# Another share of the work by seven products in the first two blocks of an RWKV layer and its feed-forward layer on Trainium2

## The chip, the cores and the metric

The kernel runs on one core of a Trainium2 chip. The metric is the device time of one execution in microseconds (us). The core's engines appear in the profile as PE (TensorE, matrix products and transposes), PEld (its weight loads), DVE (VectorE), ACT (ScalarE), POOL (GpSimd) and SP (SyncE, which only issues DMAs here). DMAs are also issued on ACT's and POOL's queues.

## The reference

All is fp32, on x with 2048 tokens of 512 numbers. First comes an RWKV layer on the layer norm of x, added to x, then a feed-forward layer on the layer norm of that, added too.

```
z  = layernorm(x)
h  = layernorm(z) * g1 + b1;  hh = h moved by one token
k, v, r = mix_k(h, hh) @ Wk.T, mix_v(h, hh) @ Wv.T, mix_r(h, hh) @ Wr.T
x1 = z + (sigmoid(r) * wkv(k, v)) @ Wo.T           # time mix
h  = layernorm(x1) * g2 + b2; hh = h moved by one token
x2 = x1 + sigmoid(mix_cr(h, hh) @ Wcr.T) * (silu(mix_ck(h, hh) @ Wkey.T) @ Wval.T)   # channel mix
y  = x + x2
out = y + (silu(gate) * up) @ w_down.T,  gate, up = split(layernorm(y) @ w_gate_up.T)
```

Wk, Wv, Wr, Wo and Wcr are 512 x 512, Wkey is 2048 x 512 and Wval 512 x 2048; the feed-forward layer is 2048 wide. mix is `h*m + hh*(1-m)` with one m for each feature.

## The kernel before

The 2048 tokens are four blocks of 512. A block's product with a 512 x 512 piece of weights is a **unit**. There are two kinds. `plain_unit` (L636) makes 32 matmuls of 128 x 128 by 128 x 256, in four quads of eight, from the weights as they lie in memory. `unit` (L541) works by seven products of half size (Winograd's form of Strassen's algorithm), 7 x 4 = 28 matmuls at L560; for this it needs four sums of weight quarters (S1 to S4) and four sums of operand quarters (T1 to T4, `sums_of`, L466, on DVE) and puts the products together with copies on ACT (`accv` L580, `u` L591, `accx` L595) and additions on DVE. An fp32 matmul leaves two records on PE in the trace. The last three products of a unit are `held`: the unit that follows pops them between its own. A plain unit with `hold` leaves its last two quads in the same way.

The weight sums are made once, in the background, by `prepare` (L147): four loads of quarters on POOL's queue (L152), four operations on DVE (L389), and behind each a write of the sum to DRAM on POOL's queue (L163). The quarters lie either in `q` buffers (30 of them, which the units use too) or in six `raw` buffers of their own. `prepare_all(weights, own, depth)` gives the order; with depth 2 the next weight's quarters are loaded while the one before is summed, with depth 1 only behind it. PE's operands come through a ring of twelve buffers that SP's queue fills in the order of use (`ring`, L166, L168), weights and sums alike; a read of a sum that isn't written yet holds up all reads behind it.

The order of PE, DVE and ACT is written out when the kernel is built, by a small planner. After every product `tick` (L297) adds share x 1.72 us to an account (`slack`) and lets background work run until the estimated DVE cost of it (`cost`, L208) has used the account up. Background work is norms, mixes and residuals, pushed as generators, and the steps of `prepare`, which are paced by `credit`: each tick adds `credit[1]`, and each step costs 1. `share` is SHARE0 up to the first up unit and SHARE behind it. So a larger share or credit moves instructions forward on all three engines, whether or not what they wait for comes sooner.

Norm 1, the time-mix norm of the second block, is `time_norm(1)` (L757): moments on DVE (L403, L404), variance and a column `shift` (L393, L397), `pow` on POOL (L413), four h on DVE (L393), then sixteen transposes on PE (L445) and ACT's evacuations to hT. For blocks 2 and 3 the norm is done on transposed input (`turned_norm`, L783): the statistics go to DRAM (L795), come back as rows by two DMAs on ACT's queue (L804), DVE applies them to xT (L389), and ACT writes hT (L816).

The units run in this order: k, r, v, out of block 0; k, r, v of block 1; then for each block b gate, out of block b+1, four up units, one down unit over the four pieces of Wval, and k, r, v of block b+2; then the feed-forward layer (gate, up and down units, L1214 among them). k, r, v and out of block 0 and k of block 1 are plain. `first_block` (L824) starts with norm 0 and its transposes, behind 24 transposes that warm PE up (L345).

Of the kernel before, what the change touches and what calls it, by code (L numbers as in the profile page):

```python
# [22 lines left out]
WAIT = 5  # L23
STEP = 1.72
SHARE = 0.88
SHARE0 = 0.95
WARM = 24
PP0 = -1e38

# [4 lines left out]
WK, WV, WR, WO, WCR = range(5)  # L34

TURNED = 2
PLAIN = {(0, WK), (0, WR), (0, WV), (0, WO), (1, WK)}
WKEY = 5
WVAL = 9
WG = 13  # L40
# [22 lines left out]
def rwkv_ffn_kernel(  # L63
# [32 lines left out]
    def q_tile(name):  # L96
        return pools["q"].tile([P, 2, HB], F32, tag="q", name=name)
# [49 lines left out]
    def prepare(n, own):  # L147

        raw = []
        for k in range(4):  # L150
            t = prep.tile([P, 2, HB], F32, tag="raw", name="raw") if own else q_tile("q")
            paced(nc.gpsimd.dma_start(flat(t), sources[n][k]))  # L152
            raw.append(t)
        yield 1
        a11, a12, a22, a21 = raw
        for k, o, i0, i1, op in (
            (0, a22, a21, a22, ALU.add),
            (2, a21, a11, a21, ALU.subtract),
            (1, a11, a22, a11, ALU.subtract),
            (3, a12, a12, a11, ALU.subtract),  # L160
        ):
            tt(o, i0, i1, op)
            nc.gpsimd.dma_start(sums[n][k], flat(o))  # L163
            yield
# [37 lines left out]
    slack = [0.0]  # L202
    share = [SHARE0]
    put_off = deque()
# [6 lines left out]
    def later(fn, ticks=1):  # L211
        put_off.append([ticks - 1, fn])
# [4 lines left out]
    def flush():  # L217
        while put_off:
            flush_one()
# [31 lines left out]
    credit = [0.0, 0.0]  # L251
# [17 lines left out]
    def begin(item):  # L269
        if not item[4]:  # L270
            item[4] = True
            next(item[2])
            item[1] = WAIT

    def prepare_all(ns, own, depth):
        empty = not preps
        for n in ns:
            preps.append([n, 0, prepare(n, own), depth, False])
        if empty:
            for item in list(preps)[:depth]:  # L280
                begin(item)
# [34 lines left out]
    def push(name, gen, ready=None):  # L316
        background.append([ready, gen, name, False, background])
# [4 lines left out]
    def need(name):  # L322
        while name not in finished:
            run_one(True)
        slack[0] = min(slack[0], 0.0)
        spent[0] = 0.0
# [61 lines left out]
    def tt(out, a, b, op):  # L388
        nc.vector.tensor_tensor(out, a, b, op)  # L389
        cost(size(out))  # L390

    def ts(out, *args):
        nc.vector.tensor_scalar(out, *args)  # L393
        cost(size(out), 0.1, 0.00085)

    def stt(out, *args):
        nc.vector.scalar_tensor_tensor(out, *args)  # L397
        cost(size(out))
# [89 lines left out]
    def mix(key, hT, row, plain=False):  # L488
        m, B = op_tile("mix")
        B["key"] = key  # L490
        ops[key] = B

        def dst(c):
            k = c // 2
            return m[:, 2 * k : 2 * k + 2, c % 2, :]

        def shifted(c):
            nc.scalar.activation(
                dst(c),
                hT[:, c, 0:TB].rearrange("p (j t) -> p j t", j=2),  # L500
                AF.Copy,
                scale=onem[:, row - MK, c : c + 1],
            )

        def mixed(c):
            stt(
                dst(c),
                hT[:, c, 1:].rearrange("p (j t) -> p j t", j=2),
                vcol(row, c),
                dst(c),  # L510
                ALU.mult,
                ALU.add,
            )

        shifted(0)
        shifted(1)
        yield 1
        for c in range(NC):
            mixed(c)
            if c + 2 < NC:  # L520
                shifted(c + 2)
            yield
        finished.add(B["key"])
        if not plain:
            yield from sums_of(B)
# [188 lines left out]
    def product_of(b, n, name, sink, by_token, done=None, free=op_done):  # L714
        if (b, name) not in ops:
            flush()
        plain = (b, n) in PLAIN
        B = Lazy((b, name), plain)
        if name != "g":
            need((b, name))  # L720
        if plain:
            plain_unit(
                n,
                B,
                sink,
                by_token,
                done,
                free,
                second_half if (b, name) == (0, "k") else None,
                (b, n) == (1, WK),  # L730
            )
        else:
            unit([n], [B], sink, by_token, done, free)
# [176 lines left out]
    def time_mix(b, name):  # L910
        row, n = {"k": (MK, WK), "r": (MR, WR), "v": (MV, WV)}[name]
        yield from mix((b, name), hTs[b, "a"], row, (b, n) in PLAIN)

# [8 lines left out]
    def k_unit(b):  # L922
        q = qs[b] = {}

        def sink(i, j, c):
            r = q_tile("r")
            for o in range(2):
                n = 2 * i + o

                ts(r[:, o, :], c[:, o, :], nfirst[:, n : n + 1], 0.0, ALU.subtract, ALU.min)  # L930
            e = q_tile("e")
            q[i, j] = e
            nc.scalar.activation(e, r, AF.Exp)
            nc.scalar.activation(r, r, AF.Exp, scale=-1.0)


            later(lambda: stt(e, e, 0.5, r, ALU.mult, ALU.mult), 2)

        product_of(b, WK, "k", sink, False)
# [20 lines left out]
    def v_unit(b):  # L960
# [5 lines left out]
        def done():  # L966
            hidden_sums((b, "g"), q, (b, WO) in PLAIN)

        product_of(b, WV, "v", sink, False, done)

    def block_view(t, i, j):
        return t[:, 2 * j : 2 * j + 2, i * HB : (i + 1) * HB]

    def out_unit(b):
        need(("x1", b))

        def sink(i, j, c):
            v = block_view(x1s[b], i, j)
            tt(v, c, v, ALU.add)

        product_of(b, WO, "g", sink, True, free=None)
# [5 lines left out]
    def channel_norm(b):  # L987
        x1 = x1s[b]
        mv = small.tile([P, NT, 2], F32, tag="mv", name="mv")
        yield from moments(x1, mv)  # L990
        var = small.tile([P, NT], F32, tag="var", name="var")
        ts(var, mv[:, :, 1], EPS, None, ALU.add)
        rstd = small.tile([P, NT], F32, tag="rstd", name="rstd")
        yield from rsqrt(var, rstd, NT, b == 0)
        h = tok_tile("h")
        yield from scaled(x1, h, mv, rstd)
        hT = htp.tile([P, NC, TB + 1], F32, tag="hT", name="hT_b")
        hTs[b, "b"] = hT
        yield 1
        yield from shifted_norm("b", h, hT, LN2G, LN2B)  # L1000
# [322 lines left out]

    early = [WR, WV, WCR, WO] + [WKEY + g for g in range(4)] + [WVAL, WVAL + 1]
    late = [n + g for g in range(4) for n in (WG, WU)] + [("dd", A11)]
    late += [("d", k) for k in range(4)] + [("dd", q) for q in (S4, S2, A12, S1, S3, A22)]

# [5 lines left out]
    second_half = first_block()  # L1335
    for n in "rv":
        push_mix(0, n, time_mix(0, n))
    credit[1] = 0.65
    k_unit(0)
    prepare_all(early, False, 2)  # L1340
    prepare_all([WVAL + 2, WVAL + 3] + [WK] + late, True, 1)
    xin[1] = load_x(1)
    push("norm1", time_norm(1))
    push_residual(0)
# [3 lines left out]
    r_unit(0)  # L1348
    v_unit(0)
    out_unit(0)  # L1350
    push("normb0", channel_norm(0))
    k_unit(1)
    push_mix(0, "cr", channel_mix(0, "cr"))
    push_mix(0, "ck", channel_mix(0, "ck"))
    r_unit(1)
# [1 line left out]
    for b in range(NB):  # L1357
        nxt = b + 2 < NB
        if nxt:
            xin[b + 2] = load_x(b + 2)  # L1360
        if b == NB - 1:
            load_resid(0)
        gate_unit(b)
        if b + 1 < NB:
            out_unit(b + 1)
        need((b, "ck"))
        if nxt:
            push(f"norm{b + 2}", time_norm(b + 2))
        for g in range(4):
            up_unit(b, g)  # L1370
            if b == 0:
                share[0] = SHARE
            if b == 1 and g == 0:
                credit[1] = 0.55
            if g == 0:
                if nxt:
                    push_mix(b + 2, "k", time_mix(b + 2, "k"))
                    push_residual(b + 2)
                    push_mix(b + 2, "r", time_mix(b + 2, "r"))
                if b + 1 < NB:  # L1380
                    push(f"normb{b + 1}", channel_norm(b + 1))
                if nxt:
                    push_mix(b + 2, "v", time_mix(b + 2, "v"))
                if b + 1 < NB:
                    push_mix(b + 1, "cr", channel_mix(b + 1, "cr"))
                    push_mix(b + 1, "ck", channel_mix(b + 1, "ck"))
        if b == NB - 1:
            push((0, "z", "t"), ffn_in(0), op_free)
        down_unit(b)
        if nxt:  # L1390
            for n, u in (("k", k_unit), ("r", r_unit), ("v", v_unit)):
                u(b + 2)
# [95 lines left out]
```

## Time and profile before

| | |
|---|---|
| three runs | 1239.46, 1239.35, 1240.74 us |
| median of the runs | 1239.46 us |
| profiled execution | 1238.08 us |
| its span in the trace | 1236.0 us |
| mean granted TensorE clock | 0.999 |
| DMA traffic | 294.06 MB, HBM at 237 GB/s |

The profile shows one execution of its own. The span is the time from the first to the last instruction in the trace; 2.08 us lie around it. Line numbers (L560) are those of the kernel below or above in this section; the form `out<-in` names the program's tiles. A row of a timeline has the start in the span, the time of the group, engine, line and operation, and in brackets the idle time of the engine ahead of it with what ended it.

### The profile page before, as it was taken

The numbers are of one execution on the slowest core, as the hardware profiler recorded it, in microseconds if no ns is written. First come the engines' busy times: TensorE is split into PE (matmuls) and PEld (weight loads), VectorE is DVE, ScalarE is ACT, GpSimd is POOL, SyncE is SP. The second block draws the span as 40 slices with busy tenths as digits, with TensorE's granted clock in tenths as the row PEclk, the third lists the DMA queues.
The fourth block names the chain that finished last, engine by engine and source line by source line (L and its number), as shares of the span: only waits on it lengthen the run. The fifth ranks groups of instructions, "written<-read, shape, count | busy, mean of one in ns | idle before, by whom it ended". The sixth has DMA issues, their size and how long they took to land.

```text
span 1236.0 us, 18098 instructions
## 1 busy us (share of the span) xinstructions
PE 1226.3 (99%) x6516; PEld 1099.8 (89%) x6516; DVE 714.4 (58%) x1321; ACT 359.3 (29%) x666; POOL 154.4 (12%) x278
## 2 busy tenths in 40 slices
PE   9999999999999999999999999999999999999998
PEld 8888887888888888888888888998899888998898
DVE  5888587586684757533532365556546365563466
ACT  5534252242522425202211222112221222112211
POOL 2332321222212121222000000000000000000000
PEclk9999999999999999999999999999999999999999
DMA  5779985899877887898556645895459745785576
GB/s 201 253 261 315 340 278 208 307 325 311 274 243 250 293 271 238 262 324 301 176 145 194 213 140 160 269 335 152 142 183 311 269 145 150 239 296 160 153 216 211
DMA packets 140303, 294.06 MB, mean 238 GB/s; under 512 B 17576, under 2 KB 18744, under 8 KB 138936
## 3 DMA queue, kind: packets, MB, share of 16 engines
q1 hardware_dynamic: 117168, 219.99, 56.3%
q0 software_dynamic: 21440, 70.27, 15.6%
q10 hardware_dynamic: 1608, 2.65, 0.6%
q8 instruction: 53, 0.87, 0.3%
q14 instruction: 34, 0.28, 0.1%
HBM read 250.89 MB, written 41.95 MB: 237 GB/s over the span
## 4 chain that ended last, share of the span: by engine, by line
PE 92%; issue 3%; DMA 2%; POOL 2%; DVE 1%; ACT 0%; POOLq 0%; DVEq 0%; ACTq 0%
PE ps L560 52%; PE ps L1214 14%; PE accx L560 10%; PE accv L560 10%; PE ps L662 4%; PE ps L445 1%; POOL q L152 1%; DMA row<-stats 1%; POOL sum L163 1%; DMA w<-sum 0%; DMA sum<-q 0%; DMA x<-in_x 0%; DVE h L393 0%; DVE resid L389 0%; DVE r L389 0%
## 5 line engine op out<-in xcount | busy, mean ns | idle before, releaser
L560 PE MATMUL ps<-zT,w 128*128 128x256 f32 x1280 | 289.5, 379 | 0.0
L560 PEld LDWEIGHTS ps<-zT,w 128*128 128x128 f32 x1280 | 241.9, 190 | 32.2
L560 PE MATMUL ps<-mix,w 128*128 128x256 f32 x960 | 219.7, 379 | 0.5 <-ACT u L591 0.5
L560 PEld LDWEIGHTS ps<-mix,w 128*128 128x128 f32 x960 | 182.1, 190 | 25.5 <-ACT u L591 0.9
L389 DVE TENSOR_TENSOR u<-u,accx 128x512 f32<-128x512 f32 x67 | 46.0, 686 | 120.5 <-ACT accx L595 120.4
L560 PE MATMUL ps<-w,t 128*128 128x256 f32 x456 | 102.5, 379 | 2.2 <-DVE st L403 1.8
L1214 PE MATMUL ps<-w,hid 128*128 128x128 f32 x832 | 104.5, 275 | 0.0
L1214 PEld LDWEIGHTS ps<-w,hid 128*128 128x128 f32 x832 | 99.8, 192 | 0.8
L560 PEld LDWEIGHTS ps<-w,t 128*128 128x128 f32 x456 | 86.2, 190 | 14.5 <-DVE st L403 2.1
L580 ACT COPY accv<-ps 128x512 f32<-128x512 f32 x67 | 38.2, 571 | 177.2 <-PE ps L560 177.2
L1214 PE MATMUL ps<-w,quads 128*128 128x128 f32 x704 | 89.0, 275 | 0.4 <-ACT r L1226 0.4
L1214 PEld LDWEIGHTS ps<-w,quads 128*128 128x128 f32 x704 | 84.2, 192 | 0.9 <-ACT r L1226 0.5
L595 ACT COPY accx<-ps 128x512 f32<-128x512 f32 x67 | 38.2, 571 | 153.6 <-PE ps L560 153.6
L389 DVE TENSOR_TENSOR u<-ps,u 128x512 f32<-128x512 f32 x67 | 46.2, 690 | 61.8 <-PE ps L560 61.5
L591 ACT COPY u<-ps 128x512 f32<-128x512 f32 x67 | 39.2, 585 | 123.4 <-PE ps L560 123.4
L1308 POOL DMA_DIRECT2D out<-resid x12 | 8.6, 716 | 512.1 <-DVE resid L389 512.1
L389 DVE TENSOR_TENSOR raw<-raw 128x512 f32<-128x512 f32 x88 | 60.5, 687 | 20.4 <-DMA raw<-in_wd 10.5
L1226 ACT COPY r<-ps 128x128 f32<-128x128 f32 x112 | 29.8, 266 | 142.1 <-PE ps L1214 142.1
L560 PE MATMUL accv<-zT,w 128*128 128x256 f32 x256 | 60.6, 379 | 0.0
L560 PE MATMUL accx<-zT,w 128*128 128x256 f32 x256 | 60.5, 379 | 0.0
L560 PE MATMUL ps<-w,s 128*128 128x256 f32 x256 | 58.2, 379 | 0.0
L662 PE MATMUL ps<-mix,w 128*128 128x256 f32 x256 | 56.8, 380 | 1.1 <-DVE mix L397 1.1
(168 smaller groups left out, 1658.8 us busy)
## 6 DMA issues: line engine op xcount, KB each, us to landing
w<-sum SPq DMA_DIRECT2D x316, 256.0 KB, 3.5
w<-in_w SPq DMA_DIRECT2D x253, 256.0 KB, 3.7
w<-dd SPq DMA_DIRECT2D x112, 256.0 KB, 3.7
w<-d SPq DMA_DIRECT2D x48, 256.0 KB, 3.7
raw<-in_w POOLq DMA_DIRECT2D x44, 256.0 KB, 5.7
sum<-raw POOLq DMA_DIRECT2D x44, 256.0 KB, 3.9
q<-in_w POOLq DMA_DIRECT2D x40, 256.0 KB, 5.9
sum<-q POOLq DMA_DIRECT2D x40, 256.0 KB, 4.5
```

Source lines behind the costliest of these rows:

```text
L152: paced(nc.gpsimd.dma_start(flat(t), sources[n][k]))
L163: nc.gpsimd.dma_start(sums[n][k], flat(o))
L389: nc.vector.tensor_tensor(out, a, b, op)
L445: nc.tensor.transpose(flat[:, t * P : (t + 1) * P], h[:, t, c * P : (c + 1) * P], ident)
L560: mm = nc.tensor.matmul(pz[:, m, :], lhsT=lhsT, rhs=rhs, start=first and g == 0 and m == 0 and k == 0, stop=g == last and k == 1, skip_gro ...
L580: "z", A11, B11, True, pop_held, read=lambda: nc.scalar.copy(accv, acc["z"])
L591: nc.scalar.copy(tmp["u2"], acc["z"])
L595: nc.scalar.copy(accx, acc["z"])
L662: mm = nc.tensor.matmul(acc[i, j][:, m, :], lhsT=act[:, k, lo] if by_token else wg[:, k, lo], rhs=wg[:, k, :] if by_token else act[:, k, : ...
L1214: mm = nc.tensor.matmul(dst, lhsT=x[k][:, g, :], rhs=wt[:, g, :], start=first and g == 0, stop=g == 3, skip_group_check=True,)
L1226: nc.scalar.copy(st["r"][:, m, n * P : (n + 1) * P], st["z"])
L1308: eng.dma_start(out_t[b][:, tokens, cols], rs[b][:, tokens, cols])
```

## The change

Six places are edited. SHARE0 goes from 0.95 to 1.05. k of block 1 leaves the set of plain units, and out of block 0 now has the hold. WK's sums are made first instead of behind those of Wval, and three pieces of Wval instead of two are summed in q buffers with depth 2; only the fourth goes through the `raw` buffers. The credit of a tick in the first part is 0.75 instead of 0.65, and 0.72 instead of 0.75 from the first up unit of block 0 on, where before it stayed at 0.65; from block 1's first up unit it is 0.55 as before. The channel norm of block 0 is pushed behind k of block 1 instead of ahead of it.

```diff
-SHARE0 = 0.95
+SHARE0 = 1.05
...
-PLAIN = {(0, WK), (0, WR), (0, WV), (0, WO), (1, WK)}
+PLAIN = {(0, WK), (0, WR), (0, WV), (0, WO)}
...
                 second_half if (b, name) == (0, "k") else None,
-                (b, n) == (1, WK),
+                (b, n) == (0, WO),
...
-    early = [WR, WV, WCR, WO] + [WKEY + g for g in range(4)] + [WVAL, WVAL + 1]
+    early = [WK, WR, WV, WCR, WO] + [WKEY + g for g in range(4)] + [WVAL + g for g in range(3)]
...
-    credit[1] = 0.65
+    credit[1] = 0.75
     k_unit(0)
     prepare_all(early, False, 2)
-    prepare_all([WVAL + 2, WVAL + 3] + [WK] + late, True, 1)
+    prepare_all([WVAL + 3] + late, True, 1)
...
     out_unit(0)
+    k_unit(1)
     push("normb0", channel_norm(0))
-    k_unit(1)
...
             if b == 0:
                 share[0] = SHARE
+                if g == 0:
+                    credit[1] = 0.72
```

## Prediction

> **What bounds the kernel now.** I read the page's busy times first, then the waits of PE and of SP's queue, then PE's timeline around each wait, and last the chain of waits.
>
> ```profile
> PE 1226.3 (99%) x6516; PEld 1099.8 (89%) x6516; DVE 714.4 (58%) x1321; ACT 359.3 (29%) x666; POOL 154.4 (12%) x278
> ```
>
> PE is busy 1226.3 of 1236.0 us, so an edit counts only where it changes PE's work or makes PE wait. Adding up the idle time ahead of PE's groups after the start leaves five places: 0.34 us at 28.1 (a mix), 0.46 at 42.85 (norm 1), 0.7 at 161.6 (block 2's k), and 1.93 and 0.65 at 201.6 and 205.7, where the first down unit lacks the sums of its fourth value block. Some 4.2 us is all that better timing can win. In the waits of PE and of SP's queue the largest of these and its cause stand as:
>
> ```profile
> PE ps L560 <- DVE st L403: 1.8, 1, 1.8
> ```
>
> ```profile
> SPq L168 <- DMA sum<-raw: 31.4, 3, 13.7
> ```
>
> The columns are total, count, longest. PE's wait is put down to a DVE operation that was long done; the SP row names the real one. The ring's reads stood up to 13.7 us behind one write of sums.
>
> **The sum goes against the profiled execution**, 1238.08 us (span 1236.0 and 2.08 around it), which lies 1.38 under the median of the runs, 1239.46. I work out a difference and add it to the median.
>
> **A. k of block 1 by seven: −1.73.** A plain unit is 32 matmuls and a unit of seven products 28. Each fp32 matmul has two records on PE.
>
> ```profile
> 46.95 29.36 PE ps L662 x136
> ```
>
> In this piece of the chain PE ran 136 records in 29.36 us without a break, 0.2159 us each. The change replaces 64 such records by 56: 8 × 0.2159 = 1.73 less. The unit's additions (four T, the u copies and additions, all on DVE and ACT) lie beside PE, which is ahead of them by its own units as in every other unit of seven. The hold moves to out of block 0: its last two quads are spread over k's products, the same matmuls in another order, so nothing. WK's sums are made first: four reads and four writes on POOL's queue, written by about 40 us and read by SP from about 66 us on. Three more loads pass SP's ring, 3 × 3.5 us landing, behind twelve buffers: nothing. The sums behind WK (r, v, cr, out, the first keys) come up to 12 us later than before and, in the instruction order, still at least 12 us ahead of their reads: nothing, and a few tenths if that cover fails.
>
> **B. The larger share moves norm 1's transposes: +4.1.** With SHARE0 at 1.05 the planner gives background work more room per product, and time_norm(1) reaches its transposes (L445) two steps of the planner earlier. PE's order is fixed when the kernel is built: the first four transposes now stand directly behind the last matmul of r of block 0, eight matmul pairs (16 records, 3.45 us) earlier than before. What they wait for does not come earlier. PE's timeline, then DVE's, then POOL's:
>
> ```profile
> 42.85 1.50 PE L445 MATMUL ps<-ident,h 128*128 128x128 f32 x8
> 44.19 1.89 PE L662 MATMUL ps<-mix,w 128*128 128x256 f32 x8
> ```
>
> ```profile
> 37.88 0.24 DVE L393 TENSOR_SCALAR var<-mv 128x4 f32<-128x4 f32 x2
> ...
> 40.41 1.00 DVE L393 TENSOR_SCALAR h<-x,mv,two 128x512 f32<-128x512 f32 x2 [0.22 <-POOL two L413]
> ...
> 42.53 1.00 DVE L393 TENSOR_SCALAR h<-x,mv,two 128x512 f32<-128x512 f32 x2
> ```
>
> ```profile
> 38.21 2.17 POOL L413 TENSOR_TENSOR two<-var,mhalf 128x8 f32<-128x8 f32 x1 [7.97 <-DVE shift L397]
> ```
>
> Up to var (37.88) DVE's order is unchanged and DVE is fully busy, so the chain var, pow on POOL (2.17), first h at 40.41 stands. In the new order DVE then does one h (0.46), one e (0.60), two sums of weights (0.60 and 0.72) and three more h (0.46, 0.46, 0.54): 40.41 + 3.84 = 44.25; the last transpose of the first four, which reads the fourth h, starts at about 44.29. PE is there at 39.40 (end of r's last matmul in before). Three transposes are done inside the wait (3 × 0.11): 44.29 − 39.40 − 0.33 = 4.56. Before, the same place cost 0.46, so +4.1. Queued behind the waiting transposes is all of v's first quad, and nothing gives it back: DVE's lead over PE grows by 4 us, but PE is the bound. If the 0.34 at 28.1 goes, PE only comes to this wait earlier. The orders are fixed, so only the durations can vary: bounds 3.5 (DVE 0.6 sooner, one operation) and 4.6 (all of the wait is new).
>
> **C. The clock: +2.0, bounds 0 and 2.8.** A wait of over 4 us on PE is not in the trace after the start; the longest, 1.93 us, left the granted clock at 1.00. Near rows stand at the two ends of the run. From the windows of granted clock (the column after DVE, ACT and POOL), after PE's last matmul, which ends at 1232.03:
>
> ```profile
> 1232.00:1233.00 1.00, 0.03 (x1) 0.00 (x0) 0.84 (x2) 0.00 (x0) 0.00 (x0) 1.00 0.00 0
> ...
> 1234.00:1235.00 1.00, 0.00 (x0) 0.00 (x0) 0.00 (x0) 0.00 (x0) 0.00 (x0) 0.66 0.38 114
> 1235.00:1236.00 1.00, 0.00 (x0) 0.00 (x0) 0.00 (x0) 0.00 (x0) 0.00 (x0) 0.50 0.00 0
> ```
>
> The clock is at a half 2.3 us after PE stopped. So a wait of 4.6 us is long enough, and work behind it would begin at half speed. The price is read at the start:
>
> ```profile
> 1.37 4.84 PE L345 MATMUL warm<-ident 128*128 128x128 f32 x24 [1.37 <-POOL ident masks.py:199]
> 6.04 1.06 PE L351 MATMUL accv<-ident 128*128 128x128 f32 x8
> ```
>
> Eight transposes of one shape later take 1.06 us, so one is (1.06 − 0.275) / 7 = 0.112 behind the other (0.275 is the mean of one). 24 would be 23 × 0.112 + 0.275 = 2.85, and took 4.84: 2.0 us lost until the clock was up. That is the value I take, since it is the only warming in the trace. Zero if the clock holds; half of the 5.5 us from the span's start until full pace, 2.8, if it rises late.
>
> By the Trainium skill ("TensorE: Matmul & The Clock Gate", Why this matters for your kernels) PE should have no idle gap over about 3 us, since one idle window brings the clock to a half; its Part 1 gives a window of some 3.4 us. This rule speaks against the change, and the trace's end agrees with it. One such window at half speed would lose about 1.7 us, an estimate from that page, and the sum below would be 0.3 lower.
>
> **D. Three value blocks in the q buffers: −2.58.**
>
> ```profile
> 194.52 5.34 PE L560 MATMUL ps<-w,t 128*128 128x256 f32 x24
> 201.63 1.97 PE L560 MATMUL ps<-w,t 128*128 128x256 f32 x8 [1.77 <-DVE st L403]
> ...
> 205.74 6.50 PE L560 MATMUL ps<-w,t 128*128 128x256 f32 x29 [0.41 <-DMA w<-sum]
> ```
>
> ```profile
> 196.59 0.54 POOL L163 DMA_DIRECT2D sum<-raw  x1 [4.84 <-DVE raw L389]
> ```
>
> PE is through 24 records at 194.52 + 24 × 0.2159 = 199.70 and goes on at 201.63, 1.93 later; 0.08 and 0.57 follow (205.17 against 205.74). The third sum of the fourth value block is written at 196.59 and reaches its matmul 5.04 later, at 201.63. With the third block in the q buffers the fourth one's quarters are loaded before the third one's sums are written, and in the new order this write is issued 6 planner steps after the down unit starts instead of 11, about 10.4 us instead of 19.0. Its matmul is due 22.4 us after that start; 10.4 + 5.0 = 15.4 leaves 7 us. All 2.58 goes, and nothing else is late there. Bounds −2.58 and 0.
>
> **E. The statistics rows of block 2: +0.8, bounds −0.7 and +2.3.** In before the rows are issued at 147.48 and land 7.3 and 9.2 us later; PE waits 0.7 at 161.61.
>
> ```profile
> 147.48 0.85 ACTq L804 DMA_DIRECT2D row<-stats  x2
> ...
> 308.28 0.84 ACTq L804 DMA_DIRECT2D row<-stats  x2
> ```
>
> The new order puts both of ACT's first hT evacuations (L816) ahead of its accv copy (L580) of the unit that PE is in, so rows, xT on DVE, hT, accv, PE hang in one line. Block 3 has this order already: rows issued 308.28, xT at 313.69 and 314.97 (6.3 us), accv copied by ACT at 317.75, PE at 318.38 where 318.30 was due: no wait. With 9.2 us it would be 2.9 of wait. In the middle (7.75) it is 1.5; less the 0.7 paid now, +0.8.
>
> The first channel norm behind k starts some 4 us later; its transposes stand as many products ahead of the gate as before (DVE has one operation less between), and POOL's pow and DVE are not behind there because PE's wait in B lets them catch up: nothing, bounds 0 and 0.7. DVE is about full from 66 to 92 us (26.3 us of work in 25.9).
>
> **The sum**: −1.73 + 4.1 + 2.0 − 2.58 + 0.8 = +2.6. The profiled execution would be 1240.7, the median 1239.46 + 2.6 = 1242.1. About 0.2%, 2.48 us, is what a measurement can tell from no change, so the bounds are 1236.98 and 1241.94.
>
> **Rivals.** 1. Not slower: the clock holds through B's wait. For it: waits of up to 1.93 us did not lower it. Against it: it was down 2.3 us after PE's end. It decides at a wait somewhere between 1.9 and 4.6 us. C is 0: +0.6, 1240.1, with −0.7 in E 1238.5. Chance 0.28. 2. Faster: B does not happen since the h are ready when the transposes come. All four would have to end by 39.4, 4.8 us earlier than worked out; POOL's spans are rough, but the first h at 40.41 is a DVE record. −1.73 − 0.46 − 2.58 + 0.8 = −4.0, 1235.5. Chance 0.06. 3. The rows land at 9.2 us and more: +1.4 on the forecast, and if the clock is the upper bound 0.8 more: 1243.5 to 1244.4. Chance 0.14. 4. The change does not do what it says: the fourth value block is still late, +2.6: 1244.7. Chance 0.05. The forecast itself, 1241 to 1243, keeps 0.47.
>
> **The numbers.** 1238.5 to 1245 leaves out rival 2 and about 0.08 of the others. Faster is rival 2 alone, 0.06. Rival 1 and a little under half of the forecast lie within 0.2%: 0.46. The rest is slower, 0.48.
>
> **What would show it.** A: L662 has 64 records fewer, L560 56 more. B: PE's first group on L445 behind 39 waits 4 to 5 us for h on L393. C: the granted clock in the windows from 42 to 48 is under 1.00. D: no wait of PE between 190 and 210, and SP's row on sum<-raw far under 13.7. E: PE waits 0 to 3 us for ACT behind the rows at about 160. The prediction is wrong if PE waits anywhere else after 48 us by over 1 us, or if the transposes' wait is under 3 us.

## The result and the profile after

Five runs of the changed kernel gave 1244.30 to 1246.42 us, median 1244.68; the kernel before beside them had a median of 1240.53. The ratio is 1.0036 (95% interval 1.0025 to 1.0048): 4.15 us slower, where +2.6 was forecast. (Measured once more on another chip, in the first experiment below, the difference was 6.3 us.) The profiled execution, 1246.42 us, is the longest of the five; the other four lie between 1244.30 and 1244.80. Its page begins so, with the clock of the 40 slices:

```profile
PE 1229.4 (99%) x6508; PEld 1102.0 (89%) x6508; DVE 717.1 (58%) x1327; ACT 360.5 (29%) x669; POOL 154.1 (12%) x278
...
PEclk9999989999999999999999999999999999999999
```

PE has 8 records fewer and is busy 3.1 us longer: records at half clock last longer. Of the 40 slices only the sixth (155 to 187 us) shows the clock; a shorter fall at 44 to 47 us is lost in the rounding. The waits of PE (total, count, longest) have two new heads, and the waits for `w<-sum` are gone:

```profile
PE accv L560 <- ACT accv L580: 4.2, 1, 4.2
PE ps L445 <- DVE h L393: 3.3, 2, 2.1
```

**At 40 us**, PE's timeline and then DVE's:

```profile
40.85 0.33 PE L445 MATMUL ps<-ident,h 128*128 128x128 f32 x1 [1.29 <-DVE h L393]
43.23 1.39 PE L445 MATMUL ps<-ident,h 128*128 128x128 f32 x3 [2.05 <-DVE h L393]
44.41 3.27 PE L662 MATMUL ps<-mix,w 128*128 128x256 f32 x8
```

```profile
38.23 0.24 DVE L393 TENSOR_SCALAR var<-mv 128x4 f32<-128x4 f32 x2
...
40.25 0.55 DVE L393 TENSOR_SCALAR h<-x,mv,two 128x512 f32<-128x512 f32 x1 [1.65 <-POOL two L413]
40.71 0.69 DVE L397 SCALAR_TENSOR_TENSOR e<-sg,e 128x512 f32<-128x512 f32 x1
41.31 1.41 DVE L389 TENSOR_TENSOR q<-q 128x512 f32<-128x512 f32 x2
42.64 1.45 DVE L393 TENSOR_SCALAR h<-x,mv,two 128x512 f32<-128x512 f32 x3
```

The first h starts at 40.25, only 0.16 us sooner than before, one e and two sums of weights stand ahead of the other three, and PE's transposes follow one h each. From start to start of PE's records the idle time here is 1.45 + 2.27 + 0.35 + 0.35 = 4.42 us. The eight records behind it take 3.27 us, where eight took 1.89 before: half clock.

**At 160 us**, ACT, then DVE, then PE:

```profile
149.80 0.93 ACTq L804 DMA_DIRECT2D row<-stats  x2
...
161.49 0.81 ACT L816 ACTIVATE hT_a<-xT,vec 128x512 f32<-128x512 f32 x1 [6.01 <-DVE xT L389]
162.82 0.81 ACT L816 ACTIVATE hT_a<-xT,vec 128x512 f32<-128x512 f32 x1 [0.51 <-DVE xT L389]
163.54 0.58 ACT L580 COPY accv<-ps 128x512 f32<-128x512 f32 x1
```

```profile
157.20 0.69 DVE L389 TENSOR_TENSOR xT<-xT,row 128x512 f32<-128x512 f32 x1 [8.68 <-DMA row<-stats]
160.77 2.02 DVE L389 TENSOR_TENSOR xT<-xT,row 128x512 f32<-128x512 f32 x3 [2.88 <-DMA row<-stats]
```

```profile
164.17 3.78 PE L560 MATMUL accv<-mix,w 128*128 128x256 f32 x8 [4.17 <-ACT accv L580]
```

The chain is rows, xT, hT, accv, PE. The second row is used 10.97 us after the issue of the pair, where the prediction's bounds came from 6.3 and 9.2. ACT's accv copy reads a product that PE has long finished, but stands behind two hT in ACT's order; PE waits 4.34 us and then runs at half clock, 3.0 us more.

The profiled executions differ by 1246.42 − 1238.08 = 8.34 us. The table counts idle time from start to start of PE's records:

| term | predicted | in the profile after |
|---|---|---|
| A, 8 records | −1.73 | −1.73 |
| B, wait for h | +4.1 | 4.42 − 0.46 = +3.96 |
| C, clock behind it | +2.0 | +1.54 |
| wait at 28.1 | (only moved) | −0.34 |
| D, fourth value block | −2.58 | −2.58 |
| E, wait for the rows | +0.8 | 4.34 − 0.72 = +3.62 |
| clock behind E | (rival 3) | +3.00 |
| one new wait at 123.6 | 0 | +0.25 |
| first product 0.34 later, 0.31 more behind the last matmul | not in it | +0.65 |
| sum | +2.6 | +8.4 |

### The profile page after: what moved, and what is told of

Same layout as the page of the kernel before. It is cut to its first block, busy times and chain, and to the rows that moved or that the text cites. A ratio compares the mean times of both kernels' runs of the same rounds, so it can differ in the third digit from the quotient of the medians.

```text
span 1244.3 us, 18098 instructions
## 1 busy us (share of the span) xinstructions
PE 1229.4 (99%) x6508; PEld 1102.0 (89%) x6508; DVE 717.1 (58%) x1327; ACT 360.5 (29%) x669; POOL 154.1 (12%) x278
## 4 chain that ended last, share of the span: by engine, by line
PE 96%; DMA 1%; DVE 1%; issue 1%; POOL 1%; ACT 0%; ACTq 0%; DVEq 0%; POOLq 0%
PE ps L560 55%; PE ps L1214 14%; PE accv L560 11%; PE accx L560 11%; PE ps L662 3%; PE ps L445 1%; DMA row<-stats 1%; POOL q L152 0%; DMA x<-in_x 0%; DVE resid L389 0%; DVE r L389 0%; DVE xT L389 0%; POOL two L413 0%; DVE h L393 0%; DVE q L389 0%
## 5 line engine op out<-in xcount | busy, mean ns | idle before, releaser
L560 PE MATMUL ps<-mix,w 128*128 128x256 f32 x1000 | 229.7, 380 | 0.0
L560 PEld LDWEIGHTS ps<-mix,w 128*128 128x128 f32 x1000 | 190.8, 191 | 26.2
L389 DVE TENSOR_TENSOR raw<-raw 128x512 f32<-128x512 f32 x80 | 54.9, 686 | 17.7 <-DMA raw<-in_w 6.9
L389 DVE TENSOR_TENSOR hid<-hid 128x512 f32<-128x512 f32 x84 | 56.6, 687 | 1.1
```

The lines of the kernel that those rows point to most:

```text
L560: mm = nc.tensor.matmul(pz[:, m, :], lhsT=lhsT, rhs=rhs, start=first and g == 0 and m == 0 and k == 0, stop=g == last and k == 1, skip_gro ...
```

## The experiments

**Theory 1**: two inputs reach PE late, h of norm 1 and the rows of block 2, and each wait brings the clock down; the rest of the change is a gain of some 5 us. **Theory 2**: the loss is spread over the DMA queues and DVE, and these two are only where it shows.

**The changed kernel again.**

> The changed kernel once more, for a second profile of it. Theory 1 (two inputs come late, h of norm 1 and the rows of block 2, and each wait brings the TensorE clock down for a while): waits on PE of about 4.4 us at 41 to 44.5 and of 3 to 4.5 us at 160 to 164, each with a piece at half clock behind it unless the clock's own timing spares one of them; 1244.5, 4 above before. Theory 2 (the loss is spread: more loads and earlier preparation fill the DMA queues, and PE waits in many places): waits elsewhere, and these two shorter or at other places.

1245.40 us, ratio 1.0050 (1.0036 to 1.0064). The second profile has 4.41 us of wait for h and 1.42 of half clock behind it, 3.57 us behind the rows (issued 151.20, second one used 161.40, 10.2 us later) and 1.63 of half clock. The waits are where theory 1 has them; the clock's share differs from run to run.

**Transposes later.**

```diff
-        if b == 1:
+        for _ in range(5 if b == 1 else 0):
             yield 1
```

> Only PE's transposes of norm 1 stand twelve matmuls (24 records, 5.2 us) later. Theory 1: the wait of 4.4 us and the half clock behind it (1.5 us) go, the wait for the rows stays: after less 5.9, some 1238.7, 1.8 under before. Theory 2: less than 2 us is won, since DVE and the queues are as late as before and PE waits at the next place.

1242.82 us, ratio 1.0031 (1.0021 to 1.0042): 2.6 under the changed kernel on the same chip, not 5.9. The wait for h, now at 46.7, is 0.92 us and without half clock. But PE now waits 2.21 us for the gate's mix. Its timeline, then DVE's:

```profile
104.65 2.98 PE L560 MATMUL ps<-w,mix 128*128 128x256 f32 x8 [2.04 <-DVE mix L397]
```

```profile
101.57 0.69 DVE L389 TENSOR_TENSOR u<-u,accx 128x512 f32<-128x512 f32 x1 [0.89 <-ACT accx L595]
102.64 0.69 DVE L389 TENSOR_TENSOR u<-ps,u 128x512 f32<-128x512 f32 x1 [0.38 <-PE ps L560]
103.25 0.68 DVE L389 TENSOR_TENSOR q<-q 128x512 f32<-128x512 f32 x1
103.85 2.73 DVE L397 SCALAR_TENSOR_TENSOR mix<-hT_b,vec,mix 128x512 f32<-128x512 f32 x4
```

Half clock adds 1.7. Seen alone this speaks for theory 2. In the order on DVE two additions to u and a weight sum stand between the gate's hT and its mix; in the changed kernel there is one e. So two things come together: PE is due at the place 5.1 us sooner than in the changed kernel (102.44 against 107.56) while DVE's mix starts only 1.7 sooner (103.85 against 105.55), and this edit put the mix behind more work.

**Rows used later.**

```diff
-        for _ in range(3):
+        for _ in range(5 if b == TURNED else 3):
             yield 1
```

(the second of the two loops in `turned_norm`)

> Only the use of the statistics rows of block 2 stands two planner steps later. Theory 1: the wait of 4.3 us behind the rows goes with the half clock behind it (3.0 in the profile, less in other executions): after less 4.5 to 7, 1237.5 to 1240; the rows still land 7 to 11 us after their issue. Theory 2: k of block 2 becomes late in its place, and less than 2 us is won.

1238.65 us, ratio 1.0000 (0.9990 to 1.0009): 6.7 under the changed kernel on the same chip, and no wait anywhere from 125 to 400 us. One line of ACT's order was worth more than all that the change gains.

**Both.**

> Both waits taken away by later use. Theory 1: what is left of the change is 8 records (1.7), the wait for the fourth value block (2.6) and the small waits of before (0.3 + 0.5 + 0.7): before less 5 to 6, some 1235, granted clock 0.999. Theory 2: not clearly under before, 1239 to 1242.

1237.25 us, ratio 0.9984 (0.9976 to 0.9993). Faster than before, but by 1.9 and not 5: the wait of 2.2 us at 104.6 and half clock (1.6) are here too.

**Transposes where the kernel before has them** (eight matmuls behind r; `range(4 if b == 1 else 0)`), rows later.

> The changed kernel with PE's transposes of norm 1 where the kernel before has them, eight matmuls behind r of block 0, and the rows' use two planner steps later. Theory 1: the wait for h is 0.5 to 1 us and leaves the clock up, so DVE gets no time to catch up, but the gate's mix has one DVE operation less ahead of it than in the run with both moved, and is late by under 0.5; before less 4 to 5.5, ratio 0.9965. Theory 2: the 2 us at 104 come back, and it is as fast as that run, ratio 0.9985.

1235.38 us, ratio 0.9965 (0.9952 to 0.9977), 3.6 under the kernel before: the number that theory 1 named, and a version that beats both kernels. PE's timeline at the place:

```profile
42.60 2.93 PE L445 MATMUL ps<-ident,h 128*128 128x128 f32 x16
46.56 3.72 PE L662 MATMUL ps<-mix,w 128*128 128x256 f32 x16 [1.02 <-ACT sg L946]
```

The waits are 1.0 for h and 1.3 for a bank (a buffer of PE's results) that ACT's sg still reads, none of over 0.7 us behind them, and the clock stays full until PE is done. The run before differs by one planner step alone. That step decides what stands ahead of the gate's mix on DVE, here one e:

```profile
101.39 0.69 DVE L397 SCALAR_TENSOR_TENSOR e<-sg,e 128x512 f32<-128x512 f32 x1 [1.09 <-ACT sg L946]
102.00 1.41 DVE L397 SCALAR_TENSOR_TENSOR mix<-hT_b,vec,mix 128x512 f32<-128x512 f32 x2
```

The first mix is done at 102.69 instead of 104.54, and PE comes at 104.02 instead of 102.44. Had PE come at 102.44, this mix would have been some 0.25 us late, not 2.2: the order on DVE is most of the wait at 104.6.

**One part alone: the share.** `SHARE0 = 1.05` in the kernel before.

> The kernel before with SHARE0 at 1.05 alone. Theory 1: the first transposes of norm 1 move behind r of block 0 here too, wait about 4.4 us and bring the clock down for one to two windows: before plus 5 to 6.5, and the rows of block 2 keep their order, with at most 1 us of wait. Theory 2 (the share is harmless, the loss comes from k by seven): within 1 us of before.

1244.60 us, ratio 1.0040 (1.0025 to 1.0054). It has the wait of 4.4 us at 41 with 1.3 of half clock, and only 1.4 us at the rows, whose order is that of before. So the share makes B, not the seven products. It has no wait at 195 to 206 either, but there PE had already come some 8 us later than in the kernel before.

**The share undone.** `SHARE0 = 0.95` in the changed kernel.

> The changed kernel with SHARE0 back at 0.95. Theory 1: no long wait at 41 and none behind the rows, but the channel norm of block 0 now reaches its transposes only where the gate starts, so PE waits there for transposes, hT and the mix, some 6 us at about 105, and loses 2 more to the clock: before plus 3 to 5. Theory 2: with the share undone the change's gain of 4.3 stands: before less 4.

1247.48 us, ratio 1.0061 (1.0046 to 1.0076): slower still than the change. The channel norm's transposes now stand directly at the gate:

```profile
105.38 4.32 PE L445 MATMUL ps<-ident,h 128*128 128x128 f32 x16 [4.04 <-DVE h L393]
...
112.01 2.47 PE L560 MATMUL ps<-w,mix 128*128 128x256 f32 x5 [2.31 <-issue]
```

The second wait is put down to "issue"; DVE's first mix ran from 111.16 to 111.85, just ahead of it. There are two waits of 4.2 and 2.6 us and 13.7 us at half clock. So the rest of the change needs the larger share, and the same share spoils norm 1. That was not in the prediction. Which of the other edits needs it (the additions of k by seven, the faster credit, the later push of the channel norm) no run separates.

**One part alone: three value blocks in the q buffers**, in the kernel before.

```diff
-[WVAL, WVAL + 1]
+[WVAL + g for g in range(3)]
...
-    prepare_all([WVAL + 2, WVAL + 3] + [WK] + late, True, 1)
+    prepare_all([WVAL + 3] + [WK] + late, True, 1)
```

> The kernel before with one part of the change alone: three value blocks in the q buffers, the fourth alone in its own. Theory 1: the waits of 1.93 and 0.65 us at 201 to 206 go and nothing else moves: before less 2.6, ratio 0.998. Theory 2 (the queue only shifts the wait to a later sum): within 0.5 us of before.

1240.89 us, ratio 1.0009 (1.0000 to 1.0019). Neither theory: the wait is there and longer. PE, then POOL's queue, then DVE:

```profile
203.25 1.97 PE L560 MATMUL ps<-w,t 128*128 128x256 f32 x8 [3.28 <-DMA w<-sum]
```

```profile
194.17 0.55 POOL L152 DMA_DIRECT2D raw<-in_w  x1 [2.31 <-DMA sum<-raw]
196.69 0.55 POOL L152 DMA_DIRECT2D raw<-in_w  x1 [1.97 <-DVE raw L389]
197.23 1.08 POOL L163 DMA_DIRECT2D sum<-raw  x2
```

```profile
195.71 1.41 DVE L389 TENSOR_TENSOR raw<-raw 128x512 f32<-128x512 f32 x2
```

When the third block is done, depth 2 starts the loads of the weight after next, and the six `raw` buffers hold one and a half weights: the loads wait for buffers that the fourth block still uses, and its last two writes stand behind them on POOL's queue. That holds up the first of the two by 0.8 us at most, since DVE makes its sum only at 195.71 to 196.40. Against the kernel before it is issued 0.64 us later (197.23 against 196.59) and takes 6.0 us to its matmul instead of 5.0: the wait grows from 1.9 to 3.4. The q buffers alone do not bring the fourth block's sums forward. (Block 3's rows cost 2.2 us there as well, at 321.)

**Two blocks in the q buffers, all else of the fast version kept.**

> The fast version of this study (transposes of norm 1 as before, rows' use later) with two value blocks in the q buffers instead of three, all else kept. Prediction's step D (the q buffers remove the wait): PE waits 2 to 3 us for the fourth block's sums at about 195 to 205 again, 1237.5 to 1238. Rival (the credit, which runs the preparation earlier, removes it): no wait there, within 0.5 of 1235.4.

1235.81 us, ratio 0.9978 (0.9969 to 0.9987), no wait between 190 and 208 us. The rival holds: without the q buffers' part the wait is gone too. SP's reads still stand 14 us behind a write of sums, so the SP row that the prediction took as the sign of this wait shows no wait of PE by itself:

```profile
SPq L168 <- DMA sum<-raw: 14.0, 1, 14.0
```

**Fewer loads beside the rows**, in the changed kernel.

```diff
+        if b == TURNED:
+            credit[0] -= 3
         nc.scalar.copy(sb[:NT, : 2 * P], pt[:NT, : 2 * P])
```

> The changed kernel with one edit: three credits are taken from the preparation of weights just before the statistics rows of block 2 are sent, so four loads of 256 KB and some writes of sums are issued some 7 us later. Orders of ACT and PE around the rows are kept. Theory: the rows land late because they share the DMA engines with these loads; without them they land 6 to 7 us after the issue, PE's wait behind them falls from 3.6 to 4.3 us to under 1.5, and the clock holds there: after less 3 to 6, some 1240. Rival: the ring's own reads fill the DMA engines anyway; landing 8 to 11 us and the wait of 3 to 4 us stay, within 1 of after.

At the rows the theory holds. POOL's loads in the changed kernel, then in this one, then the use of the rows in this one (issued 150.77):

```profile
148.54 2.18 POOL L152 DMA_DIRECT2D q<-in_w  x4
```

```profile
156.01 2.17 POOL L152 DMA_DIRECT2D q<-in_w  x4 [7.77 <-PE ps L560]
```

```profile
155.46 2.76 DVE L389 TENSOR_TENSOR xT<-xT,row 128x512 f32<-128x512 f32 x4 [7.97 <-DMA row<-stats]
```

With the loads 7.5 us later the first row is used 4.7 us after the issue of the pair and the second directly behind it, instead of 11.0, and PE does not wait at 160. The order on ACT is the same. The edit moved two writes of sums along with the four loads; the run does not tell them apart. But the time is 1247.07 us, ratio 1.0066 (1.0051 to 1.0081), against 1240 expected: what the preparation gave up here it lacked later.

```profile
PE ps L560 <- DMA w<-sum: 4.7, 1, 4.7
```

That is the fourth value block again, at 204 to 209, with 2.1 us lost to half clock.

**A slower credit**: the version with both later, and `credit[1] = 0.65`.

> Both inputs used later (norm 1's transposes twelve matmuls behind r, rows two planner steps later) and the credit of the first part back at 0.65, so that fewer steps of preparation stand ahead of the gate's mix on DVE. Expected: no wait of 2 us at 104, 0.9 at 46, and no wait for the fourth value block, since the credit is 0.72 from the first up unit on: 1234 to 1235.5. Against it: the fourth block's sums are late again by 1 to 3 us, 1236 to 1238.

1245.15 us, ratio 1.0053 (1.0040 to 1.0066). Slower than both expectations. The wait at 104 is gone, as expected; the fourth value block costs 8.8 us at 198.3 to 207.1, and half clock 2.2 more:

```profile
PE ps L560 <- DMA w<-sum: 8.6, 1, 8.6
```

The expectation that the later credit of 0.72 makes up for it was wrong.

**k plain in the fast version.**

> The fast version of this study with k of block 1 plain again (and the hold back on it). Prediction's step A: 8 records more, 1.73 us, 1237.1, unless a wait changes. Rival (the four T, u copies and additions of the unit of seven cost PE waits elsewhere): within 0.7 of 1235.4, or faster.

1236.45 us, ratio 0.9982 (0.9973 to 0.9991), 0.64 over the version with two blocks from the same chip (the fast version itself ran on another one). The 8 records are there (6516 and 6508), but the idle time of PE behind 11 us adds up to 3.3 us with k plain and 4.1 with k by seven. So A is 1.73 on PE, and some 0.8 of it goes back in small waits, over half of that in one place at 333 us (321 in the fast version), far behind the unit; why is not shown. The remaining 0.3 of the difference is not traced.

## Why the prediction was right and where it failed

The time lay in the range and on the side forecast, but near the range's end, and there is luck in it: in the profiles the change costs 8.3 us where the sum said 2.6, and the second measurement of the same kernel, 1245.40, lies above 1245. Step by step:

**A** was right as PE's work. Its "nothing" for the unit's additions stays open: 0.8 us of small waits came with k by seven in the pair above, and no run shows what makes them.

**B** was right in place, cause and size (3.96 against 4.1), and the two sums and the e on DVE between the h were seen. The share alone makes it, and moving the transposes back takes it away.

**C** was right that the clock falls; behind this wait it cost 1.3 to 2.8 us in the five profiles that have it, against 2.0. The size was luck: it was read from the warming at the start, but the price comes in windows, one or two of them, and no profile shows 2.0 behind this wait. The prediction also looked for a length of wait, between 1.9 and 4.6 us, that decides; the runs show none. Its row from the end of the run, half clock 2.3 us after the last matmul, is one draw: in the 14 profiles that time is 1.4 to 4.5 us. The Trainium skill ("TensorE: Matmul & The Clock Gate", Why this matters for your kernels) was right in kind with its rule of no idle gap over about 3 us, but a gap of 2.2 us was enough elsewhere and one of 3.6 was not: the measured numbers stand in the last section.

**D** was right in size, and its reason failed: "With the third block in the q buffers ..." is neither enough (alone: 3.4 us of wait) nor needed (two blocks: none). What removes the wait in the changed kernel is how early the preparation runs: with both inputs used later a credit of 0.75 has it done and 0.65 costs 8.8 us, and in the changed kernel three credits less cost 4.9. With the larger share alone the wait was gone too, where PE came later.

**E** is the step that was mis-sized: "In the middle (7.75) it is 1.5; less the 0.7 paid now, +0.8", with +2.3 as the upper bound. It measured +3.62; PE's wait of 4.34 us is also over the prediction's own sign, 0 to 3 us. The chain and its order were right, but the second row came 11.0 and 10.2 us after the issue of the pair, outside both rows from which the bounds were taken, and the clock fell behind this wait too, 3.0 us that the sum did not have. The bounds came from two transfers whose neighbours on the DMA queues were not looked at: before, the four loads were issued 3.2 us ahead of the rows (144.31 against 147.48); after, 1.3 us ahead (148.54 against 149.80); and without them the rows were there after 4.7 to 5.4. The prediction moved the preparation earlier in D and did not ask beside what it now ran. Of the rivals the third, the rows at 9.2 us and more with 1243.5 to 1244.4, was the closest.

The channel norm was costed at nothing "because PE's wait in B lets them catch up". Nothing was right, and the reason was not: in the changed kernel the gate's first mix is done 1.3 us ahead of PE (106.24 against 107.56), and in the version without B's long wait it is 1.3 us too (102.69 against 104.02). The wait at 104.6 in two other runs comes mostly from the order on DVE.

The prediction counted five places where PE idles; the trace before has a sixth, 0.5 us at 1230.9 near the end. All profiles have it, so it takes no part in the difference.

## What to carry to other kernels

A planner's constant moves every consumer, not only the work that it was raised for: after such a change, go through the places where an in-order engine now meets its input, and shift single consumers back (here two lines gave 9 to 10 us). Moving one consumer also changes what stands ahead of the others: here one planner step too far put three operations ahead of another mix and brought a wait of 2.2 us, so try the neighbouring places too. A transfer's landing time depends on what else is sent at that moment: bound it by what the change puts beside it, not by the same transfer's rows in the old trace.

## What the runs showed of the hardware

In these runs the granted clock changes only at the edges of windows of 3.413 us that run on their own: in all 14 profiles every later change lies a whole number of windows behind the first one. What goes with a fall is how long PE idles within one window, not the length of the wait. The run with the later transposes has both cases. Its wait of 2.21 us lies with 2.09 us in one window; its wait of 3.62 us is split, 1.89 in one window and 1.73 in the next. Its windows (busy time and count of PE, PEld, DVE, ACT and POOL, then the clock, the DMA share and GB/s):

```profile
102.56:105.97 3.41, 1.37 (x6) 0.91 (x6) 3.33 (x6) 1.45 (x3) 0.54 (x1) 1.00 0.82 273
105.97:109.38 3.41, 3.41 (x10) 2.70 (x9) 3.34 (x6) 1.72 (x4) 1.45 (x3) 0.50 0.96 327
...
157.17:160.58 3.41, 1.68 (x8) 1.14 (x6) 1.64 (x3) 0.82 (x1) 0.00 (x0) 1.00 1.05 390
160.58:163.99 3.41, 1.67 (x8) 1.49 (x9) 3.38 (x6) 2.33 (x4) 0.54 (x1) 1.00 0.23 85
163.99:167.41 3.42, 3.42 (x18) 3.01 (x17) 3.29 (x7) 1.19 (x3) 2.66 (x5) 1.00 0.75 272
```

The shorter wait halved the clock of the next window, the longer one did not. Windows with 2.18 us and more of idle time always did, those up to 1.9 never; at 2.09 and 2.11 both were seen. A window at half clock ended the spell when PE was busy in it: with 0.24 us of idle time at its start it did (the second profile of the changed kernel, from 164.56), with 0.93 (its first profile) another window followed:

```profile
159.83:163.24 3.41, 0.17 (x1) 0.00 (x0) 2.44 (x4) 1.23 (x2) 0.00 (x0) 1.00 0.75 277
163.24:166.65 3.41, 2.48 (x6) 2.04 (x7) 3.29 (x7) 1.92 (x4) 0.55 (x1) 0.50 0.21 79
166.65:170.07 3.42, 3.42 (x10) 2.71 (x9) 3.38 (x7) 0.60 (x1) 1.82 (x4) 0.50 0.30 74
170.07:173.48 3.41, 3.41 (x18) 3.00 (x17) 1.66 (x3) 2.23 (x4) 1.98 (x4) 1.00 0.94 292
```

So waits of 2.2 to 4.4 us cost nothing more (2.2 and 3.4 us in the run with three value blocks alone), 1.3 to 1.7 us (one window) or 2.7 to 3.0 us (two), by where they fell, and the same kernel's executions differ by that. For the rows of 2 KB that go to 128 partitions (256 KB each), the time from the issue of the pair to the use of the second row was 5.4 to 11 us, with the DMA engines' busy share at or over 0.85 in the stretches looked at: the share does not tell the landing time.
